# Images laid out as one run per partition, and eight copies of the second group's v and thresholds, in a four-layer convolution and wavelet kernel

## The chip, the cores and the metric

The kernel runs on one core of a Trainium2 chip. The metric is the device time of one execution in microseconds. Engines are named as in the profile: PE is TensorE (PEld its weight load), DVE is VectorE, ACT is ScalarE, POOL is GpSimd, and SP is SyncE, whose queue (SPq) issues all of this kernel's transfers.

## The reference

The input is `x` of 4 images x 64 channels x 256 x 256, in float32. Four layers follow one another:

```python
# layers 0, 2 and 3: a long 2-D convolution per channel
hx = implicit_filter(z, Xw1, Xb1, Xw2, Xb2, Xw3, Xb3, Xwo, Xfreq, t, deltas)   # three sin layers, times a decay
hy = implicit_filter(z, Yw1, ...)
k = jnp.transpose(jnp.einsum('ijk,imk->ijmk', hx, hy)[0], (2, 0, 1))           # k[c] = outer(hx[:, c], hy[:, c])
y = irfft2(rfft2(x, s=(512, 512)) * rfft2(k, s=(512, 512)) / 512)[..., :256, :256]
out = y + x * bias[:, None, None]

# layer 1: thresholds in the Haar domain
f1 = haar2d(x)                               # along both axes, to the coarsest level
acc = 0
for i in range(2):
    f4 = jnp.einsum('bchw,oc->bohw', f1 * v[i], conv_w[i])     # v[i] and tau[i] are 256 x 256
    acc = acc + jnp.sign(f4) * relu(abs(f4) - tau[i])
x = haar2d(acc, inverse=True) + x
```

As v doesn't depend on the channel, the kernel multiplies by it after the mixing of channels, and it adds `f1` to `acc` before the inverse transform. Each filter is an outer product, so the kernel does each 2-D convolution as two products with Toeplitz matrices on TensorE, along rows and along columns.

## The kernel before

Two groups of two images are worked on (`GROUPS = 2`, `NB = 2`), in rounds of two channels (`CI = 2`, so `M = 4` images of 256 x 256 a round and 32 rounds a group, 64 in all). Stage A does layer 0 and the forward transform, with 12 main pieces a round. Stage B does the mixing and thresholds of layer 1 for a group. Stage C does the inverse transform and layers 2 and 3, with 16 main pieces a round. `beside` deals the pieces of a second stage evenly between those of the first, so stage B of group 0 runs beside stage A of group 1, and stage B of group 1 beside stage C of group 0.

A round's images are loaded from the input as it comes, by image:

```python
    def load_x(t):
        grp, c0 = t // ROUNDS, t % ROUNDS * CI
        xs = big("in", f"x_{t}", 3)
        for n in range(M):
            src = x[grp * NB + n % NB, c0 + n // NB].rearrange("(k p) j -> p k j", p=P)
            nc.sync.dma_start(xs[:, 2 * n : 2 * n + 2], src)
        return xs
```

The filters of three layers come from small networks; the first runs alone at the start, the other two beside stage A. A filter row of 384 values (256 and zeros) is written 24 times in a row to DRAM, so that one strided read gives a Toeplitz tile:

```python
        def front(d):
            ps = mps.tile([P, n, N], F32, tag="ps", name=f"mlp_ps{ls[0]}{d}")
            u, k = part("u"), part("k")
            for e, l in enumerate(ls):
                # ... matmul with w1_sb (d == 0) or with wbd_sb[l] into ps
            for e, l in enumerate(ls):
                nc.vector.tensor_scalar(u[:, e, :], ps[:, e, :], cols_sb[:, l, d : d + 1], cols_sb[:, l, 3:4], ALU.add, ALU.mult)
            nc.vector.tensor_scalar(k, u, INV_2PI, ROUND, ALU.mult, ALU.add)
            nc.vector.tensor_scalar(k, k, ROUND, None, ALU.subtract)
            for c in (C1, C2, C3):
                nc.vector.scalar_tensor_tensor(u, k, -c, u, ALU.mult, ALU.add)
            nc.vector.tensor_scalar(u, u, PI, -PI, ALU.min, ALU.max)
        # ... back(): sine on ACT

    def spread(l, q):
        begin = q * QUARTER if (l, q) != (0, 0) else FIRST * CI       # QUARTER = 16 channels
        for w in range(2):
            s = slice(w * C + begin, w * C + (q + 1) * QUARTER)
            src = filters[l][s].unsqueeze(1)
            nc.sync.dma_start(filt[l][s], src.to_broadcast([src.shape[0], REPEATS, PERIOD]))

    rest = [load_tau] + [lambda q=q: spread(0, q) for q in range(1, 4)]
    rest.append(lambda: wbd_sb.extend(...))
    rest += network([1, 2])
    rest += [lambda l=l, q=q: spread(l, q) for l in (1, 2) for q in range(4)]
    rest.append(scale_tau)
```

In stage A, ScalarE and VectorE write the transformed images of a round into `f`, which has two buffers and is stored to `coef` in DRAM two rounds later:

```python
        def product(t, j):
            ...
            if j == 0:
                s["f"] = big("out", f"f_{t}", 2)
            ...
            ps = bank(f"a3ps{j}_{t}")               # one of four PSUM banks, shared with a1ps, a2ps and stage C
            # ... matmuls of fw with haarH_sb into ps
            later(lambda: nc.scalar.activation(dst, ps, AF.Copy, scale=wcol_sb[:, m : m + 1]))

        def store(t):
            to = coef[grp][:, c0 : c0 + CI].rearrange("p c b h k -> p (c b h) k")
            nc.sync.dma_start(to, st[t]["f"])
```

`coef` is laid out [partition, channel, image, half, column], so that a round is one run of 8 KB per partition. Stage B loads, for each of 64 steps, the coefficients, `v` and the thresholds `taus` (scaled on the chip and kept in DRAM):

```python
            d["f"] = bp.tile([P, NB, W], F32, tag="ft", name=f"ft_{grp}_{s}", bufs=4)
            nc.sync.dma_start(d["f"].rearrange("p b w -> p (b w)"), rows_of(coef[grp], s))
            for name, src in (("v", v), ("tau", taus)):
                t = d[name] = bp.tile([P, 2, W], F32, tag=name, name=f"{name}_{grp}_{s}", bufs=3)
                at = src.offset + s * 4 * W
                if not packed:                                   # group 0
                    flat = bass.AP(src.tensor, at, [[0, C], [2 * W, 2], [1, 2 * W]])
                    nc.sync.dma_start(t.rearrange("p i w -> p (i w)"), flat)
                else:                                            # group 1
                    for i in range(2):
                        flat = bass.AP(src.tensor, at + i * W, [[0, C], [2 * W, 2], [1, W]])
                        nc.sync.dma_start(t[i * C : (i + 1) * C], flat)
```

The stages are joined here (`c_first` holds the first round's products of stage C, `c` its further pieces, `a_last` the last products of stage A):

```python
    cut_a, cut_c = ROUNDS * 3 * M, (ROUNDS - 2) * 4 * M
    beside(a[:cut_a], rest, 2, 3 * M)                         # side pieces: networks, spreads
    beside(a[cut_a : -6 * M], phase_b(0, False), 5 * M, 0)
    ...
    main = a_last[:1] + c_first
    for pair in zip(c[:M], a_last[1:]):
        main += pair
    main += a_last[M + 1 :] + c[M:cut_c]
    beside(main, phase_b(1, True), 5 * M, 0)
```

Of the kernel before, what the change touches and what calls it, by code (L numbers as in the profile page):

```python
# [38 lines left out]
F32 = mybir.dt.float32  # L39
# [5 lines left out]
P = 128  # L45
B, C, N = 4, 64, 256
# [5 lines left out]
PERIOD = N + P  # L52
REPEATS = 24

FIRST = 2

GROUPS = 2
NB = B // GROUPS
CI = 4 // NB
M = CI * NB  # L60
# [3 lines left out]
W = 2 * N  # L64
# [8 lines left out]

@with_exitstack
def conv_haar_kernel(
    ctx: ExitStack, tc: tile.TileContext, x, zT, w1, wbd, cols, decay, wo_first, decay_first, bias, haarW, haarH, ident, wcol, wrow, mixT, packT, v, tau, out
):
    nc = tc.nc
    ctx.enter_context(tc.manual_schedule())
# [2 lines left out]
    dram = ctx.enter_context(tc.tile_pool(name="dram", bufs=1, space=DRAM))  # L82


    coef = [dram.tile([P, C, NB, 2, N], F32, tag=f"coef{g}", name=f"coef{g}") for g in range(GROUPS)]
    mixed = [dram.tile([P, C, NB, 2, N], F32, tag=f"mixed{g}", name=f"mixed{g}") for g in range(GROUPS)]
    filt = [dram.tile([P, REPEATS, PERIOD], F32, tag=f"filt{l}", name=f"filt{l}") for l in range(NL)]
    taus = dram.tile([P, 2, 2, N], F32, tag="taus", name="taus")


    def pool(name, bufs, stack=ctx, **kw):
# [5 lines left out]
    def big(tag, name, bufs):  # L97
        return ac.tile([P, 2 * M, N], F32, tag=tag, name=name, bufs=bufs)
# [7 lines left out]
    def load_x(t):  # L106
        grp, c0 = t // ROUNDS, t % ROUNDS * CI
        xs = big("in", f"x_{t}", 3)
        for n in range(M):
            src = x[grp * NB + n % NB, c0 + n // NB].rearrange("(k p) j -> p k j", p=P)  # L110
            nc.sync.dma_start(xs[:, 2 * n : 2 * n + 2], src)
        return xs

    def load_toeplitz(l, t, bufs):
# [20 lines left out]
    def constant(name, src, shape):  # L135
        t = mp.tile(shape, F32, tag=name, name=f"{name}_sb")
        nc.sync.dma_start(t, src)
        return t
# [9 lines left out]
    def network(ls):  # L148

        n = len(ls)  # L150
        st = {}

        def part(name, width=N, bufs=1):
            return mp.tile([P, n, width], F32, tag=f"{name}{n}", name=f"{name}{ls[0]}", bufs=bufs)

        def front(d):
            ps = mps.tile([P, n, N], F32, tag="ps", name=f"mlp_ps{ls[0]}{d}")
            u, k = part("u"), part("k")
            for e, l in enumerate(ls):
                if d == 0:  # L160
                    nc.tensor.matmul(ps[:, e, :], w1_sb[:, l, :], z_sb[:, l, :], start=True, stop=True)
                else:
                    nc.tensor.matmul(ps[:, e, :], wbd_sb[l][:, d - 1, :], st["h"][:, e, :], start=True, stop=True)
            for e, l in enumerate(ls):
                nc.vector.tensor_scalar(
                    u[:, e, :], ps[:, e, :], cols_sb[:, l, d : d + 1], cols_sb[:, l, 3:4], ALU.add, ALU.mult
                )

            nc.vector.tensor_scalar(k, u, INV_2PI, ROUND, ALU.mult, ALU.add)
            nc.vector.tensor_scalar(k, k, ROUND, None, ALU.subtract)  # L170
            for c in (C1, C2, C3):
                nc.vector.scalar_tensor_tensor(u, k, -c, u, ALU.mult, ALU.add)
            nc.vector.tensor_scalar(u, u, PI, -PI, ALU.min, ALU.max)
            st["u"] = u

        def back():
            st["h"] = part("h", bufs=2)
            nc.scalar.activation(st["h"], st["u"], AF.Sin)

        def repeated(r):  # L180

            ps = mps.tile([4 * REPEATS, N], F32, tag="ps", name=f"mlp_first{r}")
            nc.tensor.matmul(ps, wo_first_sb[:, r], st["h"][:, 0], start=True, stop=True)
            t = repeats[r]
            nc.vector.tensor_tensor(t[:, :N], ps, decay_first_sb[:, r], ALU.mult)
            for w in range(2):
                to = filt[0][w * C + r * CI : w * C + (r + 1) * CI].rearrange("c r e -> (c r) e")
                nc.sync.dma_start(to, t[w * CI * REPEATS : (w + 1) * CI * REPEATS])


        def last():
            ps = mps.tile([P, n, N], F32, tag="ps", name=f"mlp_out{ls[0]}")
            for e, l in enumerate(ls):
                nc.tensor.matmul(ps[:, e, :], wbd_sb[l][:, 2, :], st["h"][:, e, :], start=True, stop=True)
            padded = part("padded", PERIOD)
            nc.vector.memset(padded, 0.0)
            for e, l in enumerate(ls):
                nc.vector.tensor_tensor(padded[:, e, :N], ps[:, e, :], decay_sb, ALU.mult)
                filters[l] = padded[:, e, :]

        pieces = []
        for d in range(3):
            pieces += [lambda d=d: front(d), back]
        if ls == [0]:
            pieces += [lambda r=r: repeated(r) for r in range(FIRST)]
            pieces += [lambda r=r: first_toep.append(load_toeplitz(0, r, 4 * CI)) for r in range(FIRST)]
        return pieces + [last]
# [5 lines left out]
        nc.gpsimd.memset(t, 0.0)  # L213
    QUARTER = C // 4

    def spread(l, q):

        begin = q * QUARTER if (l, q) != (0, 0) else FIRST * CI
        for w in range(2):
            s = slice(w * C + begin, w * C + (q + 1) * QUARTER)  # L220
            src = filters[l][s].unsqueeze(1)
            nc.sync.dma_start(filt[l][s], src.to_broadcast([src.shape[0], REPEATS, PERIOD]))

    thresholds = []

# [4 lines left out]
    def scale_tau():  # L230
        wrow_sb, tau_sb = thresholds
        nc.vector.tensor_tensor(tau_sb, tau_sb, wrow_sb.unsqueeze(1).to_broadcast([P, 4, N]), ALU.mult)
        for h in range(2):
            half = tau_sb.rearrange("p (i h) k -> p i h k", h=2)[:, :, h, :]
            nc.vector.tensor_scalar(half, half, wcol_sb[:, 2 + h : 3 + h], None, ALU.mult)
        nc.sync.dma_start(taus.rearrange("p i h k -> p (i h) k"), tau_sb)

    first_x = [load_x(0)]
    haarW_sb = const.tile([P, P], F32, tag="haarW", name="haarW_sb")
# [11 lines left out]
    for p in network([0]):  # L251
        p()

    rest = [load_tau] + [lambda q=q: spread(0, q) for q in range(1, 4)]
    rest.append(lambda: wbd_sb.extend(constant(f"wbd{l}", wbd[:, l], [P, 3, P]) for l in (1, 2)))
    rest += network([1, 2])
    rest += [lambda l=l, q=q: spread(l, q) for l in (1, 2) for q in range(4)]
    rest.append(scale_tau)

    def toeplitz(ps, data, t, which):  # L260

# [60 lines left out]
    def phase_a():  # L322


        total = GROUPS * ROUNDS

# [172 lines left out]
    def phase_b(grp, packed):  # L499
# [4 lines left out]
        st = [dict() for _ in range(STEPS)]  # L504
        un = [dict() for _ in range(units)]
        pieces = []
# [6 lines left out]
        def load(s):  # L513
            if s >= STEPS:
                return
            d = st[s]
            d["f"] = bp.tile([P, NB, W], F32, tag="ft", name=f"ft_{grp}_{s}", bufs=4)
            nc.sync.dma_start(d["f"].rearrange("p b w -> p (b w)"), rows_of(coef[grp], s))
            for name, src in (("v", v), ("tau", taus)):

                t = d[name] = bp.tile([P, 2, W], F32, tag=name, name=f"{name}_{grp}_{s}", bufs=3)
                at = src.offset + s * 4 * W
                if not packed:
                    flat = bass.AP(src.tensor, at, [[0, C], [2 * W, 2], [1, 2 * W]])
                    nc.sync.dma_start(t.rearrange("p i w -> p (i w)"), flat)
                else:
                    for i in range(2):
                        flat = bass.AP(src.tensor, at + i * W, [[0, C], [2 * W, 2], [1, W]])
                        nc.sync.dma_start(t[i * C : (i + 1) * C], flat)

        def weights(u, name):
            t = st[u // 2][name]
# [126 lines left out]
    def phase_c():  # L659

        total = GROUPS * ROUNDS
        alone = total - ROUNDS
        st = [dict() for _ in range(total)]
        pieces = []
# [102 lines left out]

        def store(t):  # L770
            grp, c0 = t // ROUNDS, t % ROUNDS * CI
            for n in range(M):
                dst = out[grp * NB + n % NB, c0 + n // NB].rearrange("(k p) j -> p k j", p=P)
                nc.sync.dma_start(dst, st[t]["o"][:, 2 * n : 2 * n + 2])
            st[t].clear()

        def convolve(t, j):
# [64 lines left out]
    cut_a, cut_c = ROUNDS * 3 * M, (ROUNDS - 2) * 4 * M  # L842
# [3 lines left out]
    bp = pool("b", 2, during)  # L846
# [5 lines left out]
    during.close()  # L852
    bp = pool("b2", 2, during)
    bps = pool("bps2", 2, during, space=PSUM)
    main = a_last[:1] + c_first
    for pair in zip(c[:M], a_last[1:]):
        main += pair
    main += a_last[M + 1 :] + c[M:cut_c]
    beside(main, phase_b(1, True), 5 * M, 0)
    during.close()  # L860
    wp = pool("w", 2)
# [111 lines left out]
```

## Time and profile before

| | |
|---|---|
| time, median of 3 runs | 2852.61 us (2849.38 to 2852.84) |
| span of the profiled run | 2848.8 us |
| TensorE busy, share of the span | 2779.0 us, 98% |
| mean granted TensorE clock | 0.995 |
| DMA, over the span | 657.81 MB, mean 231 GB/s |
| stage A of group 0 (with start and filters) | up to about 500 us |
| stage B of group 0 beside stage A of group 1 | about 500 to 1150 us |
| stage B of group 1 beside stage C of group 0 | about 1215 to 2060 us |
| stage C alone | from there to the end |

The slices of the span show the stages: each digit is the busy share of a fortieth of the span (71 us), in tenths, where 9 stands for 90% or more.

```profile
PE   7999989999999999999999999999999999999999
DVE  4576643787887888368888888888756655666664
POOL 4777756788888888857777777777775544445550
GB/s 193 232 195 198 221 231 225 330 327 319 318 318 323 326 323 310 167 267 274 265 263 275 264 276 271 260 280 265 229 163 134 137 139 144 151 138 137 134 134 81
```

A line of the list of waits, such as "PE a1ps L264 <- ACT f L381: 15.1, 4, 6.4", reads: TensorE's instruction that writes `a1ps` at line 264 waited for ScalarE's that writes `f` at line 381, for 15.1 us in total, 4 times, 6.4 us at the longest. The transfers that the change touches, from the page (KB each, median us from issue to landing):

```profile
x<-in_x SPq DMA_DIRECT2D x256, 256.0 KB, 6.1
coef<-f SPq DMA_DIRECT2D x64, 1024.0 KB, 5.1
out<-o SPq DMA_DIRECT2D x256, 256.0 KB, 3.3
v<-in_v SPq DMA_DIRECT2D x64, 512.0 KB, 6.5
```

The filter transfers `filt<-padded` are 22 of 576 KB with a median of 10.4 us, and two of 432 KB.

### The profile page before, as it was taken

To read this page: it belongs to the slowest core of one execution; us is meant where nothing else is said; L and a number is where in the kernel's file an instruction comes from. 1 tells how busy PE (TensorE), PEld (TensorE's weight loads), DVE (VectorE), ACT (ScalarE), POOL (GpSimd) and SP (SyncE) were. 2 spreads that over 40 slices of the span, in tenths; PEclk is the share of its full clock that TensorE was granted. 3 is DMA by queue.
4 is the path that set the end of the run, shared out by engine and by line. 5 is a ranking of instruction groups with operands and counts; after the bars stand their busy time and mean duration, and the time that the engine had idled before them with its cause. 6 is when DMAs were issued, how large, how long until landed. Compare 5 with 4: busy or idle time off the path is not lost.

```text
span 2848.8 us, 48030 instructions
## 1 busy us (share of the span) xinstructions
PE 2779.0 (98%) x16940; PEld 2413.2 (85%) x16940; DVE 1964.0 (69%) x3461; ACT 1391.5 (49%) x1987; POOL 1959.4 (69%) x2486
## 2 busy tenths in 40 slices
PE   7999989999999999999999999999999999999999
PEld 6989978777777777888888888888899999999998
DVE  4576643787887888368888888888756655666664
ACT  2344423555555555357777777777722122212211
POOL 4777756788888888857777777777775544445550
PEclk9999999999999999999999999999999999999999
DMA  7966998999899998499999999999754444444442
GB/s 193 232 195 198 221 231 225 330 327 319 318 318 323 326 323 310 167 267 274 265 263 275 264 276 271 260 280 265 229 163 134 137 139 144 151 138 137 134 134 81
DMA packets 372847, 657.81 MB, mean 231 GB/s; under 512 B 33758, under 2 KB 273919, under 8 KB 356224
## 3 DMA queue, kind: packets, MB, share of 16 engines
q1 hardware_dynamic: 372608, 654.74, 75.7%
q8 instruction: 136, 2.23, 0.3%
q14 instruction: 103, 0.84, 0.1%
HBM read 438.60 MB, written 216.01 MB: 230 GB/s over the span
## 4 chain that ended last, share of the span: by engine, by line
PE 79%; DVE 7%; DMA 4%; issue 3%; POOL 3%; ACT 2%; SPq 0%; DVEq 0%; ACTq 0%; POOLq 0%
PE c1r L264 8%; PE c1c L264 8%; PE c2c L264 8%; PE c2r L264 8%; PE f L555 5%; PE a1ps L264 5%; PE f L544 5%; PE a2ps L264 5%; PE c2c L265 4%; PE c1c L265 4%; PE c1r L265 4%; PE c2r L265 4%; PE a3ps L372 3%; PE a1ps L265 2%; PE a2ps L265 2%
## 5 line engine op out<-in xcount | busy, mean ns | idle before, releaser
L568 ACT ACTIVATE m<-f 128x1024 f32<-128x1024 f32 x256 | 262.6, 1026 | 428.8 <-DVE f L559 394.0
L575 DVE TENSOR_TENSOR f<-f,tau 128x1024 f32<-128x1024 f32 x256 | 314.9, 1230 | 165.7 <-ACT f L571 165.7
L559 DVE TENSOR_TENSOR f<-f,v 128x1024 f32<-128x1024 f32 x256 | 314.3, 1228 | 57.9 <-PE f L544 43.3
L264 PE MATMUL a1ps<-toep,x 128*128 128x256 f32 x1024 | 313.1, 388 | 18.3 <-ACT f L381 15.1
L578 DVE SCALAR_TENSOR_TENSOR m<-f,m 128x1024 f32<-128x1024 f32 x256 | 311.0, 1215 | 0.0
L264 PE MATMUL c2r<-toep,cy 128*128 128x256 f32 x1024 | 309.1, 384 | 0.0
L264 PE MATMUL c2c<-toep,ch 128*128 128x256 f32 x1024 | 309.1, 384 | 0.0
L264 PE MATMUL c1c<-toep,ch 128*128 128x256 f32 x1024 | 309.1, 384 | 0.0
L753 ACT COPY ch<-c2r 128x512 f32<-128x512 f32 x256 | 149.3, 585 | 322.8 <-PE c2r L265 322.0
L264 PE MATMUL a2ps<-toep,ay 128*128 128x256 f32 x1024 | 305.9, 381 | 0.0
L753 ACT COPY ch<-c1r 128x512 f32<-128x512 f32 x256 | 149.2, 586 | 306.9 <-PE c1r L265 305.9
L555 PE MATMUL f<-ft,mix 128*128 128x512 f32 x512 | 248.2, 607 | 21.9 <-DVE m L578 21.2
L571 ACT ACTIVATE f<-f 128x1024 f32<-128x1024 f32 x256 | 262.8, 1026 | 0.0
L381 ACT ACTIVATE f<-a3ps,wcol_sb 128x512 f32<-128x512 f32 x196 | 130.8, 685 | 254.7 <-PE a3ps L372 144.8
L352 DVE SCALAR_TENSOR_TENSOR x<-x,bias_sb,a2ps 128x512 f32<-128x512 f32 x256 | 188.2, 743 | 65.5 <-PE a2ps L265 47.5
L599 POOL TENSOR_TENSOR gt<-gt,ft 128x1024 f32<-128x1024 f32 x64 | 151.4, 2366 | 118.3 <-ACT gt L595 118.3
L767 DVE SCALAR_TENSOR_TENSOR o<-cy,bias_sb,c2c 128x512 f32<-128x512 f32 x256 | 188.4, 742 | 64.0 <-PE c2c L265 63.6
L299 POOL TENSOR_TENSOR i<-g 128x8 f32<-128x8 f32 x63 | 13.8, 219 | 317.7 <-DMA g<-mixed 317.6
L299 POOL TENSOR_TENSOR i<-i,g 128x16 f32<-128x16 f32 x378 | 206.8, 547 | 26.0
L273 POOL TENSOR_TENSOR fw<-x 128x1024 f32<-128x1024 f32 x64 | 121.4, 1896 | 149.3 <-DVE x L352 149.3
L265 PEld LDWEIGHTS a1ps<-toep,x 128*128 128x128 f32 x1024 | 198.7, 194 | 28.2
L599 POOL TENSOR_TENSOR gt<-gt,other 128x1024 f32<-128x1024 f32 x64 | 151.4, 2366 | 99.7 <-ACT other L595 99.4
(103 smaller groups left out, 7285.4 us busy)
## 6 DMA issues: line engine op xcount, KB each, us to landing
toep<-filt SPq DMA_DIRECT2D x768, 128.0 KB, 4.5
x<-in_x SPq DMA_DIRECT2D x256, 256.0 KB, 6.1
coef<-f SPq DMA_DIRECT2D x64, 1024.0 KB, 5.1
ft<-coef SPq DMA_DIRECT2D x128, 512.0 KB, 6.4
mixed<-gt SPq DMA_DIRECT2D x128, 512.0 KB, 4.4
g<-mixed SPq DMA_DIRECT2D x64, 1024.0 KB, 7.9
out<-o SPq DMA_DIRECT2D x256, 256.0 KB, 3.3
v<-in_v SPq DMA_DIRECT2D x64, 512.0 KB, 6.5
```

The lines of the kernel that those rows point to most:

```text
L264: nc.tensor.matmul(ps[:, m, :], data[:, 0, cut], t[:, which, :], start=True, stop=False)
L265: nc.tensor.matmul(ps[:, m, HALF:], data[:, 1, cut], t[:, which, :HALF], start=False, stop=True)
L299: engine.tensor_tensor(even, s, d, ALU.add)
L555: nc.tensor.matmul(un[u]["f4"][:, j, :], mixers[0][:, u % 2, :], f[:, j, :], start=True, stop=True)
L559: nc.vector.tensor_tensor(f4, f4, weights(u, "v"), ALU.mult)
L568: nc.scalar.activation(un[u]["m"], un[u]["f4"], AF.Sign)
L571: nc.scalar.activation(un[u]["f4"], un[u]["f4"], AF.Abs)
L575: nc.vector.tensor_tensor(f4, f4, weights(u, "tau"), ALU.subtract)
L578: nc.vector.scalar_tensor_tensor(un[u]["m"], un[u]["f4"], 0.0, un[u]["m"], ALU.max, ALU.mult)
L599: nc.gpsimd.tensor_tensor(g, g, st[s][name], ALU.add)
L753: later(lambda: nc.scalar.copy(y, ps))
L767: later(lambda: nc.vector.scalar_tensor_tensor(o, old, bias_sb[:, at : at + 1], ps, ALU.mult, ALU.add))
```

## The change

Four things change.

1. The input `x` and the output lie in DRAM as `coef` does: group, partition, channel, image, half, column. The rearrangement is done outside the timed program. A round's images are then one run of 8 KB per partition, and one transfer loads or stores them; the first round's load and the last round's store stay in four pieces.
2. For the second group, `v` comes as an input `v2` in eight copies in DRAM, in the order in which the partitions want it, and the scaled thresholds are written to `taus2` in eight copies by 16 transfers of 256 KB. Each load of a step is one transfer instead of two, and eight partitions read one copy, where 64 read the same address before.
3. The networks' pieces are three per layer instead of two, and each filter spread is cut in thirds (8 of the 24 repeats each). The side pieces of the first half of stage A rise from 21 to 54 and are dealt over the same main pieces.
4. At the joint, the first four pieces of stage C's first round go before the last products of stage A, not between them.

The change is meant to make transfers longer and fewer per byte, to spread reads of one address over several, and to keep the bursts of transfers and of VectorE work short.

```diff
     def load_x(t):
         grp, c0 = t // ROUNDS, t % ROUNDS * CI
         xs = big("in", f"x_{t}", 3)
-        for n in range(M):
-            src = x[grp * NB + n % NB, c0 + n // NB].rearrange("(k p) j -> p k j", p=P)
-            nc.sync.dma_start(xs[:, 2 * n : 2 * n + 2], src)
+        src = x[grp, :, c0 : c0 + CI].rearrange("p c b k j -> p (c b k) j")
+
+        n = 2 if t == 0 else 2 * M
+        for k in range(0, 2 * M, n):
+            nc.sync.dma_start(xs[:, k : k + n], src[:, k : k + n])
         return xs
...
-        def front(d):
+        def product(d):
...
+            st["u"], st["k"] = u, k
+
+        def reduce():
+
+            u, k = st["u"], st["k"]
             nc.vector.tensor_scalar(k, u, INV_2PI, ROUND, ALU.mult, ALU.add)
...
-            pieces += [lambda d=d: front(d), back]
+            pieces += [lambda d=d: product(d), reduce, sine]
...
-    def spread(l, q):
+    def spread(l, q, part=slice(0, REPEATS)):
...
-            nc.sync.dma_start(filt[l][s], src.to_broadcast([src.shape[0], REPEATS, PERIOD]))
+            times = part.stop - part.start
+            nc.sync.dma_start(filt[l][s, part], src.to_broadcast([src.shape[0], times, PERIOD]))
...
+    def copy_tau(k):
+        tau_sb = thresholds[1]
+        for i in range(2):
+            at = taus2.offset + (i * COPIES + k) * 2 * W
+            to = bass.AP(taus2.tensor, at, [[4 * W * COPIES, C], [W, 2], [1, W]])
+            nc.sync.dma_start(to, tau_sb[:, 2 * i : 2 * i + 2].rearrange("p h k -> p (h k)"))
...
-    rest = [load_tau] + [lambda q=q: spread(0, q) for q in range(1, 4)]
+    thirds = [slice(k, k + REPEATS // 3) for k in range(0, REPEATS, REPEATS // 3)]
+    rest = [load_tau] + [lambda q=q, k=k: spread(0, q, k) for q in range(1, 4) for k in thirds]
     rest.append(lambda: wbd_sb.extend(constant(f"wbd{l}", wbd[:, l], [P, 3, P]) for l in (1, 2)))
     rest += network([1, 2])
-    rest += [lambda l=l, q=q: spread(l, q) for l in (1, 2) for q in range(4)]
+    rest += [lambda l=l, q=q, k=k: spread(l, q, k) for l in (1, 2) for q in range(4) for k in thirds]
     rest.append(scale_tau)
+    rest += [lambda k=k: copy_tau(k) for k in range(COPIES)]
...
-            for name, src in (("v", v), ("tau", taus)):
-
+            for name, src in (("v", v2), ("tau", taus2)) if packed else (("v", v), ("tau", taus)):
                 t = d[name] = bp.tile([P, 2, W], F32, tag=name, name=f"{name}_{grp}_{s}", bufs=3)
-                at = src.offset + s * 4 * W
-                if not packed:
-                    flat = bass.AP(src.tensor, at, [[0, C], [2 * W, 2], [1, 2 * W]])
-                    nc.sync.dma_start(t.rearrange("p i w -> p (i w)"), flat)
+                if packed:
+
+                    at, by_partition = s * 4 * W * COPIES, [[2 * W, 2 * COPIES], [0, C // COPIES]]
                 else:
-                    for i in range(2):
-                        flat = bass.AP(src.tensor, at + i * W, [[0, C], [2 * W, 2], [1, W]])
-                        nc.sync.dma_start(t[i * C : (i + 1) * C], flat)
+
+                    at, by_partition = s * 4 * W, [[0, C], [2 * W, 2]]
+                flat = bass.AP(src.tensor, src.offset + at, by_partition + [[1, 2 * W]])
+                nc.sync.dma_start(t.rearrange("p e w -> p (e w)"), flat)
...
-    main = a_last[:1] + c_first
-    for pair in zip(c[:M], a_last[1:]):
+    main = a_last[:1] + c_first + c[:M]
+    for pair in zip(c[M : 2 * M], a_last[1:]):
         main += pair
-    main += a_last[M + 1 :] + c[M:cut_c]
+    main += a_last[M + 1 :] + c[2 * M : cut_c]
```

Left out: the store `out`, cut like the load with `n = 2` for the last round, and the host's rearrangement of `x`, `v2` and the output.

More of the change, by code (lines that the diff above doesn't have):

```diff
@@ L55 @@
 FIRST = 2
+COPIES = 8
 GROUPS = 2
@@ L75, in conv_haar_kernel @@
 def conv_haar_kernel(
-    ctx: ExitStack, tc: tile.TileContext, x, zT, w1, wbd, cols, decay, wo_first, decay_first, bias, haarW, haarH, ident, wcol, wrow, mixT, packT, v, tau, out
+    ctx: ExitStack, tc: tile.TileContext, x, zT, w1, wbd, cols, decay, wo_first, decay_first, bias, haarW, haarH, ident, wcol, wrow, mixT, packT, v, v2, tau, out
 ):
@@ L88, in conv_haar_kernel @@
     taus = dram.tile([P, 2, 2, N], F32, tag="taus", name="taus")
+    taus2 = dram.tile([C, 2, COPIES, 2, W], F32, tag="taus2", name="taus2")
     def pool(name, bufs, stack=ctx, **kw):
@@ L173, in front, with sine @@
             nc.vector.tensor_scalar(u, u, PI, -PI, ALU.min, ALU.max)
-            st["u"] = u
-        def back():
+        def sine():
             st["h"] = part("h", bufs=2)
@@ L771, in store @@
             grp, c0 = t // ROUNDS, t % ROUNDS * CI
-            for n in range(M):
-                dst = out[grp * NB + n % NB, c0 + n // NB].rearrange("(k p) j -> p k j", p=P)
-                nc.sync.dma_start(dst, st[t]["o"][:, 2 * n : 2 * n + 2])
+            dst = out[grp, :, c0 : c0 + CI].rearrange("p c b k j -> p (c b k) j")
+            n = 2 if t == total - 1 else 2 * M
+            for k in range(0, 2 * M, n):
+                nc.sync.dma_start(dst[:, k : k + n], st[t]["o"][:, k : k + n])
             st[t].clear()
@@ L927 @@
     arrays = {
-        "x": f(a["x"]),
+        "x": f(a["x"].reshape(GROUPS, NB, C, 2, P, N).transpose(0, 4, 2, 1, 3, 5)),
         "zT": f(np.stack([a[p + "z"].reshape(N, EMB).T for p in CONV], axis=1)),
@@ L960 @@
         "v": by_row(v),
+        "v2": f(np.repeat(by_row(v).reshape(C, 2, 2, W).transpose(0, 2, 1, 3)[:, :, None], COPIES, axis=2)),
         "tau": by_row(tau),
@@ L967 @@
     ]
-    args.append(nc.dram_tensor("out", (B, C, N, N), F32, kind="ExternalOutput").ap())
+    args.append(nc.dram_tensor("out", (GROUPS, P, C, NB, 2, N), F32, kind="ExternalOutput").ap())
     with tile.TileContext(nc) as tc:
@@ L971 @@
     r = run_bass_kernel_spmd(nc, [{f"in_{n}": m for n, m in arrays.items()}], core_ids=[0])
-    return r.results[0]["out"]
+    out = np.asarray(r.results[0]["out"]).reshape(GROUPS, P, C, NB, 2, N)
+    return f(out.transpose(0, 3, 2, 4, 1, 5).reshape(B, C, N, N))
```

## The prediction

> **What bounds the kernel now.** I read the engine table and the slices first, then who TensorE waited for, then the granted clock around its longest waits, and last the timeline of one of them.
>
> ```profile
> PE 2779.0 (98%) x16940; PEld 2413.2 (85%) x16940; DVE 1964.0 (69%) x3461; ACT 1391.5 (49%) x1987; POOL 1959.4 (69%) x2486
> DMA  7966998999899998499999999999754444444442
> ```
>
> TensorE is busy for 2779.0 of 2848.8 us. Whatever the change does to transfers, it can win only the other 69.8 us, plus what a slow clock hides inside "busy". The DMA row is at eight or nine tenths in most of the first 28 slices, which tempts one to call the kernel DMA-bound; the stages say otherwise (columns: length, busy us and count for each engine, granted clock, DMA share, GB/s):
>
> ```profile
> core 0: us, PE busy (x) PEld busy (x) DVE busy (x) ACT busy (x) POOL busy (x), PEclk, DMA share, GB/s
> 350.00:500.00 150.00, 135.22 (x856) 125.18 (x855) 66.71 (x177) 51.54 (x96) 97.61 (x189) 0.94 0.88 225
> 500.00:1150.00 650.00, 628.06 (x3194) 472.04 (x3193) 518.71 (x494) 368.97 (x480) 568.00 (x649) 1.00 0.90 319
> 1150.00:1260.00 110.00, 103.32 (x670) 94.27 (x670) 51.87 (x84) 44.41 (x69) 74.05 (x121) 0.95 0.72 213
> 1260.00:2840.00 1580.00, 1579.18 (x10075) 1415.01 (x10074) 1111.39 (x2183) 797.26 (x1109) 979.57 (x1088) 1.00 0.70 202
> ```
>
> From 1260 us on TensorE idles 0.8 us in 1580, although the second group's mixing keeps the DMA engines at 0.95 share until 2000 us. More than half the kernel cannot be shortened by easier transfers. The idle time lies before 1260 us, and the list of waits names it:
>
> ```profile
> PE f L555 <- DVE m L578: 21.2, 38, 1.5
> PE a1ps L264 <- ACT f L381: 15.1, 4, 6.4
> PE mlp_ps L163 <- ACT h L178: 6.9, 2, 3.4
> PE a3ps L372 <- POOL fw L278: 4.8, 2, 4.4
> PE a3ps L372 <- DVE t L436: 4.0, 3, 1.4
> PE mlp_first L183 <- ACT h L178: 3.5, 1, 3.5
> PE mlp_ps L161 <- DMA w_sb<-in_w: 3.4, 1, 3.4
> PE a1ps L264 <- DMA toep<-filt: 3.2, 1, 3.2
> PE c1ps L696 <- DVE ci L301: 2.3, 1, 2.3
> ```
>
> The second line is the one a transfer causes. Three of its four waits (14.8 us) fall between 350 and 500 us, and in that window ScalarE's `f` waits in turn:
>
> ```profile
> ACT f L381 <- DMA coef<-f: 50.6, 5, 13.9
> ```
>
> `f` has two buffers; ScalarE cannot fill one until its store has landed, and TensorE then finds no free PSUM bank. The timeline of one case shows why the store is late (start, duration, idle before and releaser):
>
> ```profile
> 400.49 4.05 SPq L457 DMA_DIRECT2D coef<-f  x1
> 404.64 9.37 SPq L111 DMA_DIRECT2D x<-in_x  x4
> 416.20 1.27 ACT L381 ACTIVATE f<-a3ps,wcol_sb 128x512 f32<-128x512 f32 x2 [12.79 <-DMA coef<-f]
> 416.94 1.03 PE L264 MATMUL a1ps<-toep,x 128*128 128x256 f32 x2 [3.63 <-ACT f L381]
> ```
>
> The store was issued at 400.49, right behind a filter transfer (two of 576 KB, 398.26) and four image loads, and landed about 15.7 us later; the median is 5.1. In the same entry the matmul pair takes 1.03 us instead of 0.60: after the stall the array runs slow. The granted clock was 0.56 in 371–377, 0.72 in 416–422 and 0.60 in 462–470.
>
> [...] A filter transfer reads 16 partitions and repeats each row 24 times[...]: 576 KB land in a median 10.4 us, while a 1 MB coefficient store lands in 5.1. [...] The new images have 256 KB from partition to partition[...]; `coef` already has that pitch and its store lands in 5.1 us, so I take it as harmless. [...]
>
> **The change, part by part.** The order of instructions, read from both programs, has the same instructions on every compute engine; only the networks' pieces, the threshold scaling and one stage boundary move. DMA issues go from 1,184 printed rows to 1,209.
>
> *Images as one run.* A round's load goes from four DMAs with 1,024 runs of 1 KB to one with 128 runs of 8 KB. To price a byte I take two calm stretches: 200–280 us moves 198 GB/s at share 0.63, so 314 GB/s if full, with 60% of its bytes in 1 KB runs (image and Toeplitz, 1.5 of 2.5 MB a round); 500–1150 moves 319 at 0.90, so 354, with 22% (a round takes some 21 us there, 1.5 of 6.7 MB). Two equations, 0.6 a + 0.4 b = 3.19 and 0.22 a + 0.78 b = 2.82, give an estimate of a = 3.6 us per MB in 1 KB runs and b = 2.6 in runs of 4 KB and more. An image load then costs 1.0 us less of a round of 13.1 us. The store `out` gets the same form, but stage C runs at a DMA share of 0.44 with TensorE full: no gain.
>
> *Filters in thirds.* Bytes stay. In 350–500 us, 33.57 MB took 0.876 x 150 = 131 us of DMA time; taking off 16.3 MB in 1 KB runs (59 us) and 11.5 MB of coefficients (30 us) leaves 42 us for 5.9 MB of filters, 7.2 us per MB. One spread of 1.15 MB comes every 17.6 main pieces (370 over 21 side pieces), 0.79 MB per round of 12 pieces. A round in that stretch thus needs 1.5 x 3.6 + 2.6 + 0.79 x 7.2 = 13.7 us of DMA against 13.1 us of TensorE: saturated, and in bursts of 8 us. Afterwards pieces of 0.38 MB go out every 6.9 main pieces (370 over 54), 0.67 MB a round: 0.5 x 3.6 + 2 x 2.6 + 0.67 x 7.2 = 11.8 us of 13.1. It fits, and a burst delays a store by 2.8 us rather than 8. So the 14.8 us of stalls should go, and the slow clock with them: (1 - 0.56) x 6 + (1 - 0.72) x 6 + (1 - 0.60) x 8 = 7.5 us, some of it idle time, say 7. Of 21.8 us I count nine tenths: -19.6.
>
> *Networks in three pieces.* Three waits of 1.4 us (`a3ps` on DVE `t`) come when a burst of eight VectorE instructions, 7 us at 186.4–193.1, stands before the transposed images' sums. Split off, `product` (1 us) no longer stands with `reduce` (6 us), but `reduce` stays whole. -2 of 4.0.
>
> *Boundary at 1150–1260.* Four pieces of `c1r` matmuls (8 x 0.65 = 5.2 us) now stand before the last products of stage A, which waited 4.4 us for GpSimd. They cover that wait and the slow clock after it (0.65 over 6 us: 2.1). Against it, the last coefficient store comes only some two pieces before the second mixing starts instead of six, and its first `ft` needs store (4.8 us) and load (some 5 us): I allow 1.5 us of new wait. -5.
>
> *Eight copies.* Sixteen more DMAs of 256 KB (4.2 MB) in rounds 26 to 31, 0.92 MB a round: at 3.1 us per MB, between my two rates for 2 KB runs, 9.9 us of DMA a round, under 13.1. They make the second group's v and threshold loads one DMA of 4 KB runs instead of two of 2 KB, reading eight addresses instead of one; TensorE is full there, so nothing is gained. I allow +1.
>
> *First group's mixing.* The 21.2 us are 38 waits of at most 1.5 us for DVE, which waits 114.8 us for ScalarE in the same stretch: latency of a chain, and the order of it doesn't change. Lighter image loads touch it only where a v or `ft` load lands late. -2. *Start and end* -1.
>
> Sum: -19.6 - 2 - 5 + 1 - 2 - 1 = -28.6, from 2852.6: 2824.
>
> **Rivals.** *The bound that stays.* TensorE's stalls could be moved, not removed: the copies' writes go to `taus2` in 2 KB runs 64 KB apart[...]. [...] one or two stalls of 7 us with slow clock would return at 410–490 us: about 2838. Against it: the image loads have already freed 1.0 us a round. *A new wait at the boundary*: if `ft` comes 5 us late, TensorE also drops its clock, and the boundary gains nothing: 2829. *Everything with a transfer in it goes*: if the 21.2 us come from late v and `ft` loads after all (DMA share 0.90 speaks for it; waits of under 1.5 us, all for DVE, against), the kernel comes to 2806. *Nothing*: if the filters' rate and not their bunching delays the stores, half of the stalls stay: 2834.
>
> **Range and chances.** The rivals lie between 2806 and 2838; I take 2806 to 2842 as 8 in 10. Faster by over 2% means under 2795.6 us, -57 us: that needs nearly all the idle time, 17 us of which is the chain of network 0 at the start and 4 the end, which nothing here shortens. 0.04. Slower by 2% would need a new bound in stage C or the second mixing, where DMA has room: 0.02. Within 2%: 0.94.
>
> **What would show it.** Right: no wait of `a1ps` for `f` at 350–500 us, clock 0.99 or more there, `coef` stores landing under 10 us; `a3ps` waits on GpSimd gone; 1260 to the end as long as before; 38 or so waits of `f` on `m` still there. Wrong: a wait of L264 for `f` moved later, towards 490 us (copies); a wait of the second group's first mix for `ft`; or the first mixing shorter than 650 us by more than 5.

## The result, and the profile after

| | before | after |
|---|---|---|
| time, median | 2852.43 us (2849.38 to 2852.84, 4 runs) | 2817.45 us (2816.87 to 2818.99, 4 runs) |
| span of the profiled run | 2848.8 us | 2817.2 us |
| TensorE busy | 2779.0 us | 2769.1 us |
| TensorE idle (span less busy) | 69.8 us | 48.1 us |
| mean granted clock | 0.995 | 0.999 |
| DMA packets | 372,847 | 237,448 |

The ratio is 0.9881, with a 95% interval of 0.9863 to 0.9898: 35.0 us less, where the prediction had 28.6 us less (2824 us, 2806 to 2842). Of the 31.6 us between the two spans, 21.7 are idle time and 9.9 are busy time, most of which TensorE saves because it no longer runs matmuls at a lowered clock (0.56 to 0.72 for 6 to 8 us at a time before; 1.00 over 350–490 us now).

The list of TensorE's waits after, in us in total, times and the longest:

```profile
PE f L573 <- DVE m L596: 20.9, 38, 1.5
PE mlp_ps L169 <- ACT h L187: 6.9, 2, 3.4
PE mlp_first L192 <- ACT h L187: 3.5, 1, 3.5
PE mlp_ps L167 <- DMA w_sb<-in_w: 3.3, 1, 3.3
PE a1ps L283 <- DMA toep<-filt: 3.2, 1, 3.2
PE c1ps L714 <- DVE ci L320: 2.3, 1, 2.3
PE a3ps L391 <- DVE t L455: 1.4, 2, 1.0
PE a3ps L391 <- POOL fw L297: 1.3, 2, 0.8
```

The wait of `a1ps` for ScalarE's `f` (15.1 us before) is gone. `a3ps` waits 1.4 us for VectorE instead of 4.0, and 1.3 for GpSimd instead of 4.8. All else stands as it was, the longest line (20.9, was 21.2) included. The same four stretches as before, a little earlier on the clock (length, busy us and count for PE, PEld, DVE, ACT and POOL, granted clock, DMA share, GB/s):

```profile
350.00:490.00 140.00, 140.00 (x929) 129.73 (x928) 74.39 (x180) 56.65 (x99) 107.41 (x207) 1.00 0.74 252
490.00:1130.00 640.00, 618.39 (x3143) 464.67 (x3142) 518.91 (x495) 363.82 (x472) 561.98 (x639) 1.00 0.87 317
1130.00:1240.00 110.00, 107.68 (x709) 97.81 (x709) 57.83 (x89) 52.55 (x79) 79.19 (x123) 0.98 0.75 230
1240.00:2810.00 1570.00, 1569.18 (x10013) 1406.52 (x10012) 1101.19 (x2174) 788.02 (x1098) 969.13 (x1076) 1.00 0.66 202
```

In the first, TensorE is busy for all of 140 us at full clock, where it idled 14.8 of 150 at 0.94. The DMA engines move more (252 GB/s, was 225) in a smaller share of their time (0.74, was 0.88). Part of that is a shift: the changed kernel issues its last filter copy at 371.5 us, the kernel before at 444.9. In the last stretch nothing could be gained and nothing was: 0.8 us idle before and after, though the DMA share falls from 0.70 to 0.66. In the timeline of the changed kernel, a coefficient store at about the same time, and what follows it, now look like this (start, duration):

```profile
397.28 0.33 SPq L476 DMA_DIRECT2D coef<-f  x1
397.82 0.94 SPq L117 DMA_DIRECT2D x<-in_x  x1
397.94 0.69 ACT L400 ACTIVATE f<-a3ps,wcol_sb 128x512 f32<-128x512 f32 x1 [5.60 <-PE a3ps L391]
```

The queue issues the store in 0.33 us where it was held up for 4.05, and ScalarE waits for TensorE's product and no longer for a store. No filter copy runs at that moment, but the fourteen stores between 200 and 371 us, among the filter copies, are issued in 0.33 or 0.34 us too, and no store of the changed kernel takes longer than 7.9 us to land (17.7 before).

### The profile page after: what moved, and what is told of

It is laid out like the page before. It is cut to its first block, busy times and chain, and to the rows that moved or that the text cites. A ratio compares the mean times of both kernels' runs of the same rounds, so it can differ in the third digit from the quotient of the medians.

```text
span 2817.2 us, 47099 instructions
## 1 busy us (share of the span) xinstructions
PE 2769.1 (98%) x16940; PEld 2406.2 (85%) x16940; DVE 1964.7 (70%) x3461; ACT 1394.6 (50%) x1987; POOL 1958.0 (70%) x2486
## 2 busy tenths in 40 slices
DMA packets 237448, 661.92 MB, mean 235 GB/s; under 512 B 26622, under 2 KB 135711, under 8 KB 204704
## 4 chain that ended last, share of the span: by engine, by line
PE 85%; DVE 7%; issue 3%; ACT 2%; POOL 2%; DMA 1%; SPq 0%; DVEq 0%; ACTq 0%; POOLq 0%
PE c1r L283 8%; PE c2c L283 8%; PE c1c L283 8%; PE c2r L283 8%; PE a1ps L283 6%; PE a2ps L283 6%; PE f L573 5%; PE f L562 5%; PE c2c L284 4%; PE c1r L284 4%; PE c1c L284 4%; PE c2r L284 4%; PE a3ps L391 3%; PE a1ps L284 3%; PE a2ps L284 3%
## 5 line engine op out<-in xcount | busy, mean ns | idle before, releaser
L573 PE MATMUL f<-ft,mix 128*128 128x512 f32 x512 | 248.2, 607 | 21.6 <-DVE m L596 20.9
L318 POOL TENSOR_TENSOR i<-g 128x8 f32<-128x8 f32 x63 | 13.7, 217 | 317.2 <-DMA g<-mixed 317.1
L284 PEld LDWEIGHTS a2ps<-toep,ay 128*128 128x128 f32 x1024 | 194.6, 190 | 26.3
```

The source lines that it names most:

```text
L284: nc.tensor.matmul(ps[:, m, HALF:], data[:, 1, cut], t[:, which, :HALF], start=False, stop=True)
L318: engine.tensor_tensor(even, s, d, ALU.add)
L573: nc.tensor.matmul(un[u]["f4"][:, j, :], mixers[0][:, u % 2, :], f[:, j, :], start=True, stop=True)
```

## The experiments

Each run is compared with runs of the kernel before, made beside it on the same chip; their medians were 2851.85 us for the first four runs, 2851.14 for the second four and 2849.98 for the last four. The changed kernel was timed only beside the 2852.43 of the table, so a difference of under some 3 us between it and a run below is not resolved. "-20.5" below means 20.5 us under that median. The "rounds" are stage A's of 13.1 us of TensorE time.

**Theory.** The three long stalls come from DMA engines that are asked for more in a round than a round lasts, since the filter copies are slow (576 KB in a median 10.4 us, a coefficient store of 1 MB in 5.1). Rivals: the number of runs that the one queue must issue; the networks, which the change moved and split; and, later, the length of a burst rather than the average.

### One part at a time on the kernel before

**Images alone.** The edit is the `load_x` and `store` part of the diff, nothing else:

```diff
-            nc.sync.dma_start(xs[:, 2 * n : 2 * n + 2], src)      # four of these, 1 KB runs
+            nc.sync.dma_start(xs[:, k : k + n], src[:, k : k + n])  # one, 8 KB runs
```

> The kernel before with the new layout of images and output alone. My theory (TensorE's three stalls at 350 to 490 us come from DMA engines saturated by bursts of filter copies): a round needs 12.7 us of DMA instead of 13.7, the bursts of 1.15 MB stay, so about half of the 22 us of stalls and slow clock goes: -8 to -16 us. Rival 1 (the number of runs that the one queue must issue, 1,664 a round, holds the stores back, not the bytes): all stalls go, -20 to -24 us. Rival 2 (the moved and split networks removed the stalls): 0 to -3 us.

Measured: 2831.38 us, ratio 0.9925 (0.9911 to 0.9940), -20.5. No wait of `a1ps` for `f` is left in the profile. But the profiled execution took 2826.19 us and the other three 2831.09 to 2832.33, so a stall in those is not excluded; and even in the profile ScalarE still waits for stores:

```profile
ACT f L383 <- DMA coef<-f: 35.0, 5, 7.8
```

The gain is more than my theory had granted it (half of the stalls) and as much as rival 1 asked for. Rival 2 is out, for the networks were untouched. My estimate, from the prediction's prices, had been 12.7 us of DMA per round of 13.1, so by my own numbers the stalls had no reason to stay; I had kept half of them for the bursts.

**Filters in thirds and networks in three pieces**, alone:

```diff
-    rest += [lambda l=l, q=q: spread(l, q) for l in (1, 2) for q in range(4)]
+    rest += [lambda l=l, q=q, k=k: spread(l, q, k) for l in (1, 2) for q in range(4) for k in thirds]
```

The rest of this edit is as in the diff above.

> The kernel before with the filter copies in thirds and the networks in three pieces, images and joint as before. My theory: 12.8 us of DMA a round and bursts of a third of the length, so most stalls go, -14 to -22 us, and the waits for VectorE's network bursts lose 2 of 4 us. Rival 1 (number of runs): the image runs stay, so most stalls stay, -2 to -6 us. Rival 2 (networks): -20 to -25 us and no stall left.

Measured: 2825.71 us, 0.9909 (0.9895 to 0.9924), -26.1. Again no stall is left, with all 1,024 image runs of 1 KB a round still there. So the number of runs isn't needed to explain the stalls. This run can't tell the thirds from the networks, and rival 2 asked for nearly the same. That the stalls go without touching the networks is shown by the images above and the wide copies below; no run cuts the spreads alone. With 46 side pieces the spreads also come less densely than I had set: by the same estimate 12.1 us of DMA a round, not 12.8. It is 4 us more than I had set as the upper end; the waits for VectorE fell by 0.8 only, so that part of it isn't explained by waits.

**The joint** alone:

```diff
-    main = a_last[:1] + c_first
-    for pair in zip(c[:M], a_last[1:]):
+    main = a_last[:1] + c_first + c[:M]
+    for pair in zip(c[M : 2 * M], a_last[1:]):
```

> The kernel before with the new joint of the stages alone. My theory: the 4.4 us wait for GpSimd and 2 us of slow clock after it go, 1.5 us of new wait for the second group's first coefficients may come: -4 to -7 us. Rival (the wait only moves to the next product of stage A, as GpSimd is late anyway): 0 to -2 us.

Measured: 2845.93 us, 0.9981 (0.9974 to 0.9988), -5.9; the interval of the ratio gives -3.4 to -7.4 us. The 4.4 us wait for GpSimd is gone, and a wait of 0.8 us for `ft` from `coef` has come. The stalls in stage A are as before (17.8 us in this run).

**The same filter bytes from more partitions.** This is no part of the change, but takes what the theory holds for the cause by itself. Layers 2 and 3 need their filters only in stage C, so any order of writing will do:

```diff
-    rest += [lambda l=l, q=q: spread(l, q) for l in (1, 2) for q in range(4)]
+    rest += [lambda l=l, q=q: wide(l, q) for l in (1, 2) for q in range(4)]
+    # wide(l, q): for each half w, all 64 channels (64 partitions), repeats 6*q to 6*q+5
+    #             instead of 16 channels (16 partitions), all 24 repeats
```

> The kernel before, in which the filter copies of layers 2 and 3 read all 128 partitions, 6 of the 24 repeats at a time, instead of 16 partitions with all 24: the same bytes, the same number of pieces at the same places, the same runs of 1.5 KB. If the copies are slow because they read 16 partitions[...], their landing falls from about 10 to 5 or 6 us, the stalls at 350 to 490 us go and the time falls by 16 to 24 us. If they are slow for another reason (the repeats, the runs of 1.5 KB, the writes to DRAM), landings and stalls stay, 0 to -4 us.

Measured: 2829.48 us, 0.9920 (0.9904 to 0.9937), -22.4. Bytes, places, pieces and the 1.5 KB runs are the same. The page's list of transfers, of the kernel before and of this one (KB each, median us to landing):

```profile
filt<-padded SPq DMA_DIRECT2D x22, 576.0 KB, 10.4
```

```profile
filt<-padded SPq DMA_DIRECT2D x22, 576.0 KB, 6.8
```

The copies land in a median 6.8 us, which still mixes in six copies of the first layer; the 16 of layers 2 and 3 alone take 6.5 (10.7 before), a little over what I had expected. Each of them reads 64 partitions, the two of a piece all 128. The stalls at 350–490 us are gone; what is left of that wait, 1.8 us, lies before 150 us, where the first layer's copies still read 16 partitions. The run shows the effect of the whole shape (10.7 to 6.5 us), not that of the partitions read alone: the rows written are also cut otherwise (64 of 9 KB, not 16 of 36).

### One part taken away from the changed kernel

**Without thirds** (and with the networks in two pieces):

> The changed kernel with whole filter copies and networks in two pieces, as before; images, copies and joint stay. The three single parts have shown that any one relief of the DMA engines takes the stalls away. My theory: the image layout alone keeps them away here too, but the side pieces fall from 54 to 29 and all move later, so the writes of the threshold copies and the spreads crowd more: 2820 to 2826 us, that is 3 to 9 us more than the changed kernel, 2 of it in waits for VectorE. Rival (the parts are needed together): stalls of the a1ps matmuls for f return, 2832 us or more.

Measured: 2845.24 us, 0.9977 (0.9969 to 0.9986), only -5.9; 28 us more than the changed kernel. The stalls are back, earlier than before. The list of waits, and the stretch in which most of them lie:

```profile
PE a1ps L279 <- ACT f L396: 16.9, 7, 4.3
250.00:350.00 100.00, 88.77 (x576) 81.42 (x575) 49.61 (x140) 31.62 (x62) 64.82 (x130) 1.00 0.92 225
```

My expectation was wrong here, and the rival right that thirds and the rest belong together. The reason is in how side pieces are dealt. The eight copies of the thresholds are side pieces too. Without thirds there are 29 in all, so a whole spread of 1.15 MB comes every 370/29 = 12.8 main pieces instead of every 17.6, 1.08 MB a round. By the prediction's prices, which are estimates from the trace before, that is 0.5 x 3.6 + 2 x 2.6 + 1.08 x 7.2 = 14.8 us of DMA in 13.1. The changed kernel's images cannot pay for that. It is the place of the copies among the pieces and not their bytes: all but 1.6 us of these waits end between 276 and 361 us, and the first of the copies' sixteen writes is issued at 365.

**Without the image layout:**

> The changed kernel with images and output by image in runs of 1 KB, as before. My theory: thirds of the filters suffice in the filter rounds; where the threshold copies are written a round needs 10.9 us of DMA, which fits, so no stall: 2817 to 2822 us. Rival (images are what matters; the copies' writes are dear): stalls at 400 to 490 us, 2826 to 2835 us.

Measured: 2818.53 us, 0.9884 (0.9869 to 0.9899), no measured difference from the changed kernel, and no stall. With the other parts in place, the images aren't needed, and the sixteen writes of the copies bring no stall.

**Without the eight copies:**

> The changed kernel without the eight copies: the second group's v and thresholds load as two transfers of 2 KB runs from one address, as before, and the 16 writes are gone. My theory: TensorE is full in the second mixing, so the copies gain nothing: 2815 to 2819 us, no difference that can be measured, with the DMA share in the second mixing back at 0.95 or so. Rival (copies relieve the second mixing): 2822 us or more, with TensorE waiting in the stretch from 1240 to 2030 us.

Measured: 2819.55 us, 0.9887 (0.9872 to 0.9902), no measured difference. Between 1300 and 1900 us the DMA share is 0.957 without and 0.906 with them, and 0.950 in the kernel before, and TensorE is full in all three. The median landing of v is 8.1 us with copies (512 KB at once) and 8.0 without (256 KB, two per step).

**With the old joint:**

> The changed kernel with the joint of before. My theory: the wait for GpSimd of 4 to 6 us and the slow clock after it return: 2822 to 2825 us, 5 to 8 us more than the changed kernel. Rival (the joint gains only what stage A's stalls left over): 2817 to 2820 us.

Measured: 2825.04 us, 0.9906 (0.9890 to 0.9923), 7.6 us above the changed kernel's median; the longest wait for GpSimd is 6.0 us. It lies 6.5 us above the run without images and 5.5 above that without copies, both taken beside it. From either side, the joint is worth 5 to 8 us.

### Pace or length, source or bytes

**Whole spreads at the pace of thirds.** The changed kernel, with two empty side pieces behind each whole spread:

```diff
+    idle = lambda: None
+    spaced = lambda ops: [p for op in ops for p in (op, idle, idle)]
-    rest = [load_tau] + [lambda q=q, k=k: spread(0, q, k) for q in range(1, 4) for k in thirds]
+    rest = [load_tau] + spaced([lambda q=q: spread(0, q) for q in range(1, 4)])
```

(and the same for layers 2 and 3).

> The changed kernel with whole filter copies (1.15 MB at once), each followed by two empty side pieces, so that their pace is that of the thirds (0.67 MB a round) and everything else stays where the changed kernel has it. Theory P (pace: a round's demand on the DMA engines, 11.8 us of 13.1 here against 14.8 in the run without thirds, decides): no stalls of a1ps for f, 2816 to 2821 us. Theory L (length: a burst of 8 us holds a store back beyond its deadline whatever the average): stalls of 8 to 20 us return, 2828 to 2845 us.

Measured: 2817.71 us, 0.9884 (0.9868 to 0.9901), the same as with thirds, and no stall, although each burst is three times as long and its transfers land in a median 13.5 us. So at this load the pace decides whether TensorE stalls: with more side pieces, the same spreads come less densely. That each is short isn't needed for it, but it isn't without effect. The stretch from 250 to 350 us, first of this run and then of the changed kernel:

```profile
250.00:350.00 100.00, 100.00 (x675) 93.86 (x674) 60.19 (x156) 42.75 (x78) 75.96 (x139) 1.00 0.95 248
250.00:350.00 100.00, 100.00 (x675) 93.78 (x674) 59.97 (x156) 42.49 (x78) 76.08 (x141) 1.00 0.83 254
```

At the same pace, whole spreads keep the DMA engines busy for 0.95 of the time and thirds for 0.83. Stores issued between 200 and 380 us land in up to 15.2 us with whole spreads and in at most 5.6 with thirds. TensorE waits in neither, but the paced kernel is close to it: in the run without thirds, the stores between 300 and 380 us take 15.7 to 18.5, and there it stalls. Its share, 0.92, is lower than the 0.95 here, so the share alone doesn't tell a stall.

**Whole spreads at the crowded pace from many partitions:** the run without thirds, with `wide` for layers 2 and 3.

> The changed kernel without thirds (side pieces 29, the crowded pace at which stalls came back), with the copies of layers 2 and 3 reading all 128 partitions. If the slow source is the root of it, the same bytes at the same pace no longer saturate (0.5 x 3.6 + 2 x 2.6 + 1.08 x 3 = 10.2 us of 13.1): no stalls but perhaps one in the first layer's copies, 2819 to 2825 us. If bytes and writes to DRAM saturate, the stalls stay: 2838 to 2846 us.

Measured: 2820.73 us, 0.9897 (0.9882 to 0.9911), no wait of `a1ps` for `f` at all. The same pace and bytes that cost 28 us from 16 partitions cost 3 from 64 (against the paced run beside it, and the networks in two pieces are part of that); their copies land in 7.5 us instead of 12.0.

**Networks in two pieces:**

> The changed kernel with the networks in two pieces, as before; thirds stay. If the split shortens VectorE's bursts where it matters, the waits of a3ps for VectorE go back to 3 or 4 us from 1.4: 2819 to 2822 us. If only the places of the networks among the rounds count: 2816 to 2819 us.

Measured: 2821.95 us, 0.9903 (0.9889 to 0.9918), 4.2 us above the paced run beside it. The waits of `a3ps` are 3.1 for VectorE and 3.0 for GpSimd, against 1.3 and 1.2 in the paced run: the 3.6 us between them are most of it, though both profiled executions were the slowest of their four (2826.24 and 2820.43). The split is worth some 4 us; the run also moves the networks by a few pieces.

**The 20.9 us that are left.** The largest wait of the changed kernel is that of the first group's mixing matmuls for VectorE, which frees their PSUM tile. So I let the subtraction write to SBUF:

```diff
-            nc.vector.tensor_tensor(f4, f4, weights(u, "tau"), ALU.subtract)
+            over = un[u]["over"] = f4 if packed else bp.tile([P, 2, W], F32, tag="over", ..., bufs=1)
+            nc.vector.tensor_tensor(over, f4, weights(u, "tau"), ALU.subtract)
 ...
-            nc.vector.scalar_tensor_tensor(un[u]["m"], un[u]["f4"], 0.0, un[u]["m"], ALU.max, ALU.mult)
+            nc.vector.scalar_tensor_tensor(un[u]["m"], un[u]["over"], 0.0, un[u]["m"], ALU.max, ALU.mult)
```

> The changed kernel, in which the first group's subtraction of the threshold writes to SBUF instead of back into PSUM, so that the PSUM tile is free 1.2 us earlier, at the end of the subtraction, and no longer at the end of the product with the sign. The 38 waits of the mixing matmuls for that product, at most 1.5 us each and 20.9 in sum, should go: 2798 to 2806 us. Rival: the product then reads two operands from SBUF beside GpSimd, which is busy 88% of this stretch, and is held up: 2817 us or more, with the product longer than 1.21 us.

Measured: 2879.64 us, 1.0102 (1.0087 to 1.0117), 62 us above the changed kernel. Groups of instructions (busy us, mean ns) and waits of this run:

```profile
L597 DVE SCALAR_TENSOR_TENSOR m<-over,m 128x1024 f32<-128x1024 f32 x128 | 245.3, 1916 | 0.0
L597 DVE SCALAR_TENSOR_TENSOR m<-f,m 128x1024 f32<-128x1024 f32 x128 | 155.5, 1215 | 0.0
PE f L573 <- DVE over L594: 3.1, 5, 0.8
PE a3ps L391 <- POOL fw L297: 67.4, 27, 5.5
```

One line of its detail (ns at least, median, at most; first and last start in us):

```profile
L597 DVE SCALAR_TENSOR_TENSOR m<-over,m x128: 1208/1639/3348, 490.9 to 1183.6; 128x1024 f32<-128x1024 f32 x128
```

The wait I aimed at fell from 20.9 to 3.1 us. But the product takes a mean of 1916 ns with both operands in SBUF and 1215 with one in PSUM. The fastest of them takes 1208, so two operands in SBUF are not slow in every case. GpSimd is slowed too (its sums `f<-x` of 128 x 1024 rise from a mean of 1894 ns to 2121), and TensorE now waits 67.4 us for GpSimd. That the two engines hold each other up is my reading of the two rises; the run doesn't show it one instruction at a time. GpSimd, busy for 88% of that stretch before and 97% in this run, has less to give away than PSUM.

## Why the prediction was right

2824 us was predicted and 2817.45 measured. The steps in turn, with the sum of -28.6 against -35.0. The two profiled executions differ by 31.6: when the first mixing starts, the changed kernel is 24.2 us ahead (507.9 against 483.7 us), the mixing adds 0.4, the joint 6.8 (the second mixing starts at 1197.1 instead of 1228.5), and the rest 0.2.

**The stalls of stage A (-19.6).** Right, and the discount of a tenth was not needed: 15.1 us of waits are gone, and most of the 9.9 us of busy time too, since `a1ps` matmuls of 256 columns have a mean of 383 ns instead of 388, which is 4.8 us in 1,024, and those of 128 columns save another 2.2. The prediction's count of DMA time per round ranks the runs: the two highest have the stall, and no other has more than 1.8 us of it. Demand is worked out as in the prediction (3.6 us per MB for 1 KB runs, 2.6 for 4 KB and more, 7.2 for filters from 16 partitions; for 64 partitions I put 3; the prediction's working, done for 350–490 us of the wide run, with a share of 0.76, 242 GB/s and 10.7 rounds, leaves 17 us for 5.9 MB of filters, an estimate of 2.9); a round lasts 13.1 us. The prediction's sum has a slip: its prices are per million bytes, but it counted the round's transfers in MB of 1,048,576 bytes and the spreads in MB of 1,024,000. The second column of demand puts that right:

| run | filter MB a round | demand, as predicted (estimate, us a round) | demand, bytes put right (estimate) | wait of a1ps for f, us |
|---|---|---|---|---|
| before, and joint alone | 0.79 | 13.7 | 14.2 | 15.1 and 17.8 |
| images alone | 0.79 | 12.7 | 13.1 | 0 (in the fastest of four) |
| thirds alone (46 side pieces) | 0.57 | 12.1 | 12.6 | 0 |
| wide alone | 0.79 | 10.4 | 10.8 | 1.8, none at 350–490 us |
| after | 0.67 | 11.8 | 12.3 | 0 |
| after without thirds | 1.08 | 14.8 | 15.3 | 16.9 |
| after without thirds, wide | 1.08 | 10.2 | 10.7 | 0 |
| after, whole spreads at the pace of thirds | 0.67 | 11.8 | 12.3 | 0 |
| after without images | 0.67 | 12.8 | 13.3 | 0 |

So 13.1 is no sharp limit: images alone lies on it and the run without images just above, and neither shows a stall in its profile. Nor is the first row a test, as the price of 7.2 was read from that very stall. And for thirds that price is too high: the shares of 0.83 and 0.95 between 250 and 350 us are 10.9 and 12.4 us of a round's 13.1, where the count gives 12.3 for both.

The second reason of this step, "a burst delays a store by 2.8 us rather than 8", was true in kind, as the longest landings of 5.6 and 15.2 us show, but it didn't decide: the paced run, with bursts of full length, loses nothing. And the parts do not add: images alone give 20.5 us, thirds with networks 26.1, yet both together with joint and copies 35.0. Each of them alone had already removed the stall, the images at least in the profiled execution.

**Networks in three pieces (-2).** Right in kind and half of what it is: 2.6 us of VectorE waits are gone in the profile, and taking the split back costs some 4 us, as GpSimd's waits fall with VectorE's.

**The joint (-5).** Right: -5.9 alone, and 7.6 when taken back. The new wait for `ft` that I allowed 1.5 us for comes in some profiles (0.8 with the joint alone, 1.2, 1.6 and 2.1 in three others) and not in that of the changed kernel.

**Eight copies (+1).** No effect that can be measured, as argued. That side holds one surprise, which the prediction had not seen: as side pieces they press the others closer. With thirds that is harmless; with whole spreads from 16 partitions the stalls come back (16.9 us).

**First mixing (-2), start and end (-1).** The first is 0.3 us; the step failed in its small way, since no late v or `ft` load lay behind those 38 waits. The last run shows that PSUM's release does (the waits fall from 20.9 to 3.1 us), and that freeing it costs more than it gives (62 us more in all). Waits at the start went from 17.0 to 16.9 us.

Of the rivals, the lighter images did not let everything with a transfer in it go (2806), nor did half of the stalls stay (2834), nor did stalls move to the copies (2838, for which I had assumed dear writes that no trace shows), nor did a late `ft` undo the joint (2829).

What stays open: why thirds alone gave 26.1 us where stalls, slow clock and VectorE's waits account for some 23 (the profiled executions differ by 24.3); whether images alone stalled in the executions that were not profiled; and the price per MB of copies from many partitions, which no run isolates (2.9 is an estimate).

## What to carry to other kernels

Where the bound engine stalls in one stretch, add up what a round asks of the DMA engines there and compare it with the round's length. Such a sum ranked the kernels here, but gave no sharp limit. Once the stall was gone, further relief earned nothing here (2817.45 us with all parts, 2818.53 without the images), so three remedies for one stall did not add up. Look at which partitions a repeated copy reads before cutting it up; here the same bytes from 64 partitions instead of 16 landed in 6.5 us instead of 10.7 and removed the stalls at 350–490 us without any other edit. And pieces dealt evenly beside a main sequence share a budget: adding some anywhere changes the pace of all.

## What the runs showed of the hardware that was not expected

In the last run, a product of two operands on VectorE took a mean of 1916 ns (1208 to 3348) with both in SBUF beside a GpSimd that was busy for 97% of the stretch, and 1215 ns with one in PSUM; GpSimd's own instructions got longer (2121 ns for 128 x 1024 sums, against 1894 in the kernel before). Waits of TensorE up to 1.5 us each, 21 us in 38 of them, left its granted clock at 1.00, while four waits of 3.6 to 6.4 us in the kernel before were followed by 0.56 to 0.72 for 6 to 8 us. Length alone didn't decide: in the run without thirds the stretch of 250–350 us holds five waits, the longest 3.8 us, and its clock is 1.00.
